# Layer 0's far entries: weighing on ScalarE, a sum over a transposed view on VectorE, and a search for the largest over four blocks at once

## The chip, the cores and the metric

The kernel runs on one core of one Trainium2 chip. The metric is device time in microseconds for one execution. The kernel before takes 1902.93 us, the median of three runs (1902.68 to 1903.74).

## The reference

Four graph layers are applied one after another to `x` (2708 nodes, 128 features), all with one adjacency `adj` (2708 x 2708). About 2.4% of the entries of `adj` are nonzero: a random symmetric pattern plus the diagonal, each entry weighted by a uniform number between 0.05 and 1. After each layer the result is added to `x` and normalized. Layer 0 is the one that is changed:

```python
s = node_feats @ msg_w[:, :D].T
d = node_feats @ msg_w[:, D:].T
messages = jax.nn.gelu(s[:, None, :] + d[None, :, :] + msg_b, approximate=False)
aggregated = jnp.einsum('ijd,ij->id', messages, adj)
combined = jnp.concatenate([node_feats, aggregated], axis=-1)
new_feats = combined @ upd_w.T + upd_b
h = jax.nn.gelu(new_feats, approximate=False) + node_feats
```

So for every pair (i, j) a vector of 128 GELUs is weighted by `adj[i, j]` and summed over j. A pair whose weight is zero adds nothing.

## The kernel before

**The two ways through layer 0.** The kernel has a sparse way, which is always run, and a dense way (`all_pairs`, from line 1082), which stands in a branch at the end of the program:

```python
    with tc.If(counts[0] > 0), ExitStack() as top:
        load_x()
        all_pairs()
        layers_1_to_3(top)
```

`counts[0]` is the number `bad_n` that the sparse way leaves behind, read by `layers_1_to_3` at its beginning. If it is above zero, then after the sparse layer 0 and layers 1 to 3 have all been run, `x` is loaded anew, layer 0 is computed over all pairs, and layers 1 to 3 are run once more on it.

**The sparse way.** The rows i are cut into `LT` = 22 tiles of `LR` = 125 rows; the columns j into `NB` = 22 blocks of `JB` = 124. For each row and block the nonzero entries are ranked by position. The first `CAP` = 5 of a block go into five slots. `slot` (L836) builds one-hot matrices `S`, `pick` (L944) uses them on TensorE to gather rows of `d` (and the weights beside them, in the last 25 columns of `dA`) into PSUM tiles `sl` (three buffers) and adds `s`; ScalarE takes the GELU (L1028); VectorE makes the weights `W` (`weigh`, L1014); TensorE sums (`add_up`, L957), two blocks at a time.

**The far entries.** What lies beyond the fifth entry of a block is "far". `past` (L864) leaves the far weights of a row in `o` (128 x 2728) and the number of far entries of each block in `count`. `largest_of` (L877) takes the 8 largest of every two blocks with VectorE's MAX8 into `cand` (11 groups of 8), `largest` (L881) takes the `OV` = 16 largest of those into `v`. `where` (L908) finds their columns, `fetch` (L912) gathers rows of `d` from HBM with 16 indirect DMAs of GpSimd, which add onto the rows of `s` that `start_far` (L903) has put into `far`. `far_gelu` (L919) takes the GELU of eight at once (128 x 1024); `far_sum` (L922) adds one weighted far entry to `extra` on VectorE; `turn` (L930) brings `extra` and the slots' sums together on TensorE, and `close` copies them to `aggT`.

**The kernel's own test for lost entries.** `check` (L889) compares, for each row, the far entries that were counted with those that came out in `v`:

```python
nc.vector.tensor_reduce(n[:, 2:3], self.count, AX.X, ALU.add)
nc.vector.tensor_tensor(n[:, 2:3], n[:, 2:3], n[:, 0:1], op=ALU.subtract)
nc.vector.tensor_tensor(bad[:, self.t:self.t + 1], n[:, 2:3], n[:, 1:2], op=ALU.add)
```

`n[:, 0]` is the number of positive values in `v`, `n[:, 1]` the number of equal neighbours among them. The sum of `bad` over all rows becomes `bad_n` (L1076).

**The order of the work.** It is written out by hand. The loop over `block` (L1021, 484 blocks) emits, for block b: `pick(b)` on TensorE, the GELU of b on ScalarE, `weigh` of block b-1 on VectorE, then the steps that are due at this block, then every second block `add_up`. Steps come from `Rows.when` (L748), sorted by their block, and within a block by tile and by place in the list. Each engine works through its instructions in this order. Counted in blocks of the tile that is being picked, the far steps of that tile fall on: `where` 1 and 3, `fetch` 2 and 11, `far_gelu` 15 for its first eight entries and 28 (that is block 6 of the next tile) for the second eight; `far_sum` two at a time on 17 to 20 and on 30 to 33 (8 to 11 of the next tile); `turn` and `close` on 36 (14 of the next). Beside them lie steps of the next tile: `rank` (a matmul by `tri`, L820, and a copy by ScalarE, L821) on 1, 3, 9, 11, 17 and 18, `part0` (L828, ScalarE) on 3, 9 and 17, `rank_row` (L861) with `past` and `largest_of` on 5, 7, 13, 15, 20 and 21. `rank`, `rank_row` and `turn` share one PSUM tile `ps` (L629, one buffer): each must wait until the one before has been read out.

**The dense way.** `all_pairs` goes through the 2708 rows one by one: a GELU of 128 x 2708 on ScalarE, then for each half of the row TensorE spreads the row of `adj` over the partitions into PSUM (`bc`, two buffers of 1354 columns), and VectorE multiplies and sums:

```python
nc.vector.scalar_tensor_tensor(
    g[:, b0:b1], g[:, b0:b1], 1.0, bc[:, :b1 - b0], op0=ALU.mult, op1=ALU.mult,
    accum_out=part[:, i, h:h + 1])
```

For every 25 rows GpSimd splits the weights into three bf16 parts (five instructions over 2708 columns).

Of the kernel before, what the change touches and what calls it, by code (L numbers as in the profile page):

```python
# [14 lines left out]
F32 = mybir.dt.float32  # L15
BF16 = mybir.dt.bfloat16
U32 = mybir.dt.uint32
AF = mybir.ActivationFunctionType
ALU = mybir.AluOpType
AX = mybir.AxisListType  # L20
PSUM = bass.MemoryType.PSUM

P = 128
# [149 lines left out]
def gnn_stack(ctx: ExitStack, tc: tile.TileContext, t, out: bass.AP):  # L173
    nc = tc.nc
    N, D = t["x"].shape
# [355 lines left out]
    NB = 22  # L531
# [12 lines left out]
    PB = BANK // P  # L544
# [7 lines left out]
    with ExitStack() as l0:  # L552
# [10 lines left out]
        with ExitStack() as msg:  # L563
# [62 lines left out]
            vp = msg.enter_context(tc.tile_pool(name="values", bufs=3))  # L626
            up = msg.enter_context(tc.tile_pool(name="sums", bufs=2))
# [110 lines left out]
            class Rows:  # L738
# [9 lines left out]
                def when(self):  # L748
                    base = (self.t - 1) * NB
                    yield base + 8, self.load_s  # L750
                    for h, (b0, b1) in enumerate(thirds):
                        b = base + b0
                        yield b - 10, lambda h=h: self.load(h)
                        yield b - 1, lambda h=h: self.find(h)
                        at = (1, 3, 5, 7) if b1 - b0 == HB else (1, 2, 4, 5)
                        for n in range(2):
                            m = 2 * h + n
                            yield b + at[n], lambda h=h, n=n: self.rank(h, n)
                            yield b - 5 + 4 * n, lambda m=m: self.load_row(m)
                            yield b + at[2 + n], lambda m=m: self.rank_row(m)  # L760
                            yield b + at[2 + n], lambda m=m: self.past(m)
                            yield b + at[2 + n], lambda m=m: self.largest_of(m)
                        yield b + 9, lambda h=h: self.part0(h)
                        yield b + 10, lambda h=h: self.part1(h)
                        for k, wait in enumerate(((12, 13, 14, 15, 16), (8, 8, 9, 11, 11), (14, 15, 16, 17, 18))[h]):
                            yield b + wait, lambda h=h, k=k: self.slot(h, k)
                    b = base + NB
                    yield b, self.largest
                    yield b + 6, self.check
                    for n in range(OV // 8):  # L770
                        yield b + 1 + n * 2, lambda n=n: self.where(n)
                    if self.t == 0:
                        b += 4
                    for n in range(OV // 8):
                        yield b - 1 + n * 9, lambda n=n: self.start_far(n)
                        yield b + 2 + n * 9, lambda n=n: self.fetch(n)
                        yield b + 15 + n * 13, lambda n=n: self.far_gelu(n)
                        for k in range(8):
                            yield b + 17 + n * 13 + k // 2, lambda n=n, k=k: self.far_sum(n * 8 + k)
                    yield b + 36, self.turn  # L780
                    yield b + 36, self.close

# [81 lines left out]
                def past(self, m):  # L864
                    if m == 0:
                        self.o = op_.tile([P, max(NB * JB, NT * D)], F32, name="o")
                        self.o = self.o[:, :NB * JB].rearrange("p (b j) -> p b j", j=JB)
                        self.cand = vp.tile([P, NB // 2, 8], F32, name="cand")
                        self.count = vp.tile([P, NB], F32, name="count")
                    b = slice(m * PB, min((m + 1) * PB, NB))  # L870
                    n = b.stop - b.start
                    nc.vector.scalar_tensor_tensor(self.o[:, b, :], self.ps[m][:, :n, :JB], EDGE + CAP,  # L872
                                                   self.ar[m][:, :n, :], op0=ALU.is_ge, op1=ALU.mult)
                    nc.vector.tensor_scalar(self.count[:, b], self.ps[m][:, :n, JB], -float(CAP), 0.0,
                                            op0=ALU.add, op1=ALU.max)

                def largest_of(self, m):  # L877
                    for b in range(m * PB, min((m + 1) * PB, NB), 2):
                        nc.vector.max(self.cand[:, b // 2, :], self.o[:, b:b + 2, :].rearrange("p b j -> p (b j)"))  # L879

                def largest(self):  # L881
                    c = self.cand.rearrange("p g e -> p (g e)")
# [36 lines left out]
                def far_gelu(self, n):  # L919
                    nc.scalar.activation(self.far[n], self.far[n], AF.Gelu)  # L920

                def far_sum(self, k):  # L922
                    w, f = self.v[:, k:k + 1], self.far[k // 8][:, k % 8, :]
                    if k == 0:
                        self.extra = up.tile([P, D], F32, name="extra")
                        nc.vector.tensor_scalar(self.extra, f, w, None, op0=ALU.mult)
                    else:
                        nc.vector.scalar_tensor_tensor(self.extra, f, w, self.extra, op0=ALU.mult, op1=ALU.add)  # L928

                def turn(self):  # L930

# [81 lines left out]
            with tc.manual_schedule():  # L1013
                def weigh(b, g, sl, W):  # L1014
                    nc.vector.tensor_tensor(  # L1015
                        W[:, :, :RG].rearrange("p (k c) i -> p k c i", k=2), columns_of(sl, D, DA),
                        own[:, None, None, :].to_broadcast([P, 2, 3, RG]), op=ALU.mult)


                late = []  # L1020
                for block in range(LT * NB):  # L1021
                    i, b = divmod(block, NB)
                    while steps and steps[0][0] < block:
                        steps.pop(0)[2]()
                    sl, W = sl_all[block % len(sl_all)], W_all[block % len(W_all)]
                    R[i].pick(b, sl)
                    g = ep.tile([P, 6, D], F32, name="g")
                    nc.scalar.activation(g.rearrange("p (k c) d -> p k c d", k=2), columns_of(sl, 0, D), AF.Gelu,  # L1028
                                         scale=1.0 / D_SCALE)
                    if late:  # L1030
                        weigh(*late[-1])
                    while steps and steps[0][0] == block:
                        steps.pop(0)[2]()
                    late.append((b, g, sl, W))
                    if len(late) == LAG + 2:
                        R[(block - LAG) // NB].add_up(late[:2])
                        late = late[2:]
                weigh(*late[-1])
                R[-1].add_up(late)


                rest = [step for _, _, step in steps]
                assert len(rest) == 11
                last_gelu, far_sums, last_turn = rest[0], rest[1:9], rest[9:]
                G = len(groups())
                ahead = LR * (LT - 1) // BANK
                U.open()
                for n in range(ahead):
                    U.sums(n)
                    if n > 0:  # L1050
                        U.rows(n - 1)
                    if n == 1:
                        last_gelu()
                    if n == 2:
                        for step in far_sums:
                            step()
                for step in last_turn:
                    step()
                U.rows(ahead - 1)

                most = vp.tile([P, 1], F32, name="most")
                ones = vp.tile([P, 1], F32, name="ones")
                fine = vp.tile([P, LT], F32, name="fine")
                nc.vector.memset(ones, 1.0)
                nc.vector.tensor_tensor(fine, tot[:, :, 0], tot[:, :, 1], op=ALU.add)
                nc.vector.tensor_tensor(fine, fine, fine, op=ALU.is_equal)
                nc.vector.tensor_tensor(bad, bad, fine, op=ALU.subtract)
                nc.vector.tensor_scalar(bad, bad, 1.0, None, op0=ALU.add)
                nc.vector.tensor_reduce(most, bad, AX.X, ALU.add)

                def between():
                    ps = p_misc.tile([P, BANK // P, P], F32, name="ps")
                    nc.tensor.matmul(ps[:1, 0, :1], ones, most, start=True, stop=True)
                    for n in range(ahead, G):
                        U.sums(n)
                    nc.vector.tensor_copy(bad_n, ps[:1, 0, :1])  # L1076
                    for n in range(ahead, G):
                        U.rows(n)

                U.norm.all(between)  # L1080
# [865 lines left out]
```

## Time and profile before

| | |
|---|---|
| median of three runs | 1902.93 us |
| profiled execution, its own time | 1905.26 us |
| its span | 1903.5 us |
| TensorE busy | 1626.2 us (85%) |
| VectorE busy | 1436.1 us (75%) |
| ScalarE busy | 1052.1 us (55%) |
| GpSimd busy | 630.8 us (33%) |
| layer 0's loop over blocks | from about 55 us to about 882 us |
| layers 1 to 3 | from about 939 us to the end |
| one tile of 22 blocks in the middle of the loop | 37.0 us |

Engines are named PE (TensorE matmul), PEld (its weight load), DVE (VectorE), ACT (ScalarE), POOL (GpSimd) and SP (SyncE). L928 is line 928 of the kernel. A group of instructions is shown as "out<-in, shape, count | busy us, mean ns of one | idle time of the engine just before them, and what ended it". Two instructions of one engine can overlap at their edges, so a group's busy time can be less than its count times the mean. No instruction of lines 1082 to 1147 is in this trace.

### The profile page before, as it was taken

What the parts mean: (1) busy time and instruction counts of PE and PEld (TensorE: products, weight loads), DVE (VectorE), ACT (ScalarE), POOL (GpSimd) and SP (SyncE); (2) the same over time, 40 slices, a digit from 0 to 9 for tenths busy, and PEclk for the clock granted to TensorE, in tenths of its full rate; (3) what the DMA queues carried; (4) which work ended last, traced back from release to release, by engine and by line L of the source; (5) the groups of instructions that cost most, each with busy time, mean ns of one, the idle gap of its engine ahead of it and who ended that gap; (6) DMA issues with size and microseconds to landing.
All of it is one profiled execution on the core that took longest, in us unless ns stands there. A gap on an engine that the chain in (4) does not pass through costs nothing.

```text
span 1903.5 us, 36624 instructions
## 1 busy us (share of the span) xinstructions
PE 1626.2 (85%) x14033; PEld 955.4 (50%) x14033; DVE 1436.1 (75%) x3607; ACT 1052.1 (55%) x1538; POOL 630.8 (33%) x426
## 2 busy tenths in 40 slices
PE   5899999999999999986599997577888897199995
PEld 5666666666666666655344443322223343044542
DVE  6899999999999999986678885838886783860104
ACT  3667667666766766654444444458886771430003
POOL 5667766776776677565100000000000000000000
PEclk8899999999999999998699998658998798599997
DMA  8666665666666576533134430032334463354431
GB/s 214 153 130 143 133 144 119 148 122 141 143 131 142 122 149 124 117 69 88 63 123 150 152 112 1 1 106 76 142 137 140 141 199 146 137 204 146 146 121 31
DMA packets 234896, 238.30 MB, mean 125 GB/s; under 512 B 28844, under 2 KB 219630, under 8 KB 228122
## 3 DMA queue, kind: packets, MB, share of 16 engines
q1 hardware_dynamic: 183670, 212.18, 36.1%
q0 software_dynamic: 51040, 23.68, 10.7%
q8 instruction: 112, 1.84, 0.4%
q14 instruction: 74, 0.61, 0.1%
HBM read 220.65 MB, written 15.15 MB: 124 GB/s over the span
## 4 chain that ended last, share of the span: by engine, by line
PE 43%; DVE 28%; POOL 8%; issue 7%; ACT 7%; DMA 5%; DVEq 0%; SPq 0%; ACTq 0%; POOLq 0%
PE acc L1843 10%; POOL far L914 8%; PE lg L1231 5%; PE acc L1238 5%; PE accV L1571 5%; DVE ix L910 5%; PE ps L1499 4%; DMA far<-d_tab,ix 3%; DVE W L1015 3%; PE sl L950 3%; DVE extra L928 2%; DVE o L872 2%; DVE S L840 2%; PE accO L1575 2%; DVE dA L833 1%
## 5 line engine op out<-in xcount | busy, mean ns | idle before, releaser
L914 POOL DMA_INDIRECT far<-d_tab,ix x352 | 563.0, 1600 | 257.5 <-DVE W L1015 110.6
L1028 ACT ACTIVATE g<-sl 128x768 f32<-128x768 f32 x484 | 393.3, 813 | 257.0 <-PE sl L955 201.0
L950 PE MATMUL sl<-dA,S 124*128 124x153 f16 x4840 | 408.2, 231 | 10.1 <-DVE W L1015 7.7
L950 PEld LDWEIGHTS <-S 124*128 124x128 f16 x4840 | 330.4, 98 | 79.7 <-issue 67.9
L966 PE MATMUL acc<-g,W 128*32 128x128 f32 x4840 | 205.5, 277 | 0.5 <-issue 0.5
L966 PEld LDWEIGHTS acc<-g,W 128*32 128x32 f32 x4840 | 140.6, 109 | 58.8 <-issue 55.5
L955 PE MATMUL sl<-s,same 50*128 50x384 f16 x968 | 161.9, 308 | 0.0
L1015 DVE TENSOR_TENSOR W<-sl,own 128x150 f32<-128x150 f32 x484 | 143.4, 300 | 14.6 <-ACT g L1028 13.4
L1232 ACT ACTIVATE w<-lg,row_L_gnn_gate_bias 128x512 f32<-128x512 f32 (+1 forms) x132 | 83.5, 636 | 108.2 <-PE lg L1231 106.9
L1486 POOL TENSOR_TENSOR arena<-arena,off 128x128 f32<-128x128 f32 (+1 forms) x22 | 21.6, 982 | 351.1 <-DMA arena<-in_adjT 321.3
L840 DVE TENSOR_SCALAR S<-rk 124x1000 f16<-124x1000 bf16 (+1 forms) x330 | 133.4, 430 | 0.0
L910 DVE FIND_INDEX8 ix<-v,o 128x8 uint32<-128x2728 f32 x44 | 131.7, 2993 | 0.0
L1571 PE MATMUL accV<-arena,X 128*128 128x512 f32 (+4 forms) x264 | 124.7, 592 | 6.5 <-DVE arena L1537 6.5
L1231 PE MATMUL lg<-qT,mT 128*128 128x512 f32 (+2 forms) x264 | 121.1, 547 | 3.6 <-ACT w L1232 3.1
L1238 PE MATMUL acc<-w,both 128*128 128x512 f32 (+2 forms) x264 | 121.2, 547 | 0.0
L928 DVE SCALAR_TENSOR_TENSOR extra<-far,v,extra 128x128 f32<-128x128 f32 x330 | 114.9, 348 | 6.3
L449 DVE TENSOR_TENSOR g<-ps,row_L_gnn_b 128x512 f32<-128x512 f32 (+2 forms) x14 | 7.9, 574 | 148.1 <-PE ps L447 148.0
L1499 PE MATMUL ps<-XT 128*128 128x512 f32 (+8 forms) x150 | 90.4, 691 | 32.2 <-ACT arena L1505 26.5
L872 DVE SCALAR_TENSOR_TENSOR o<-ps,ar 128x496 f32<-128x496 f32 x132 | 82.4, 624 | 37.0 <-issue 19.7
L1843 PE MATMUL acc<-at,x 128*128 128x512 f32 (+2 forms) x156 | 66.2, 574 | 48.4 <-ACT x L379 48.4
L1233 DVE TENSOR_TENSOR w<-w,at 128x512 f32<-128x512 f32 (+1 forms) x132 | 82.5, 625 | 27.1 <-ACT w L1232 27.1
L879 DVE MAX8 cand<-o 128x8 f32<-128x248 f32 x242 | 90.4, 411 | 0.0
(357 smaller groups left out, 2507.2 us busy)
## 6 DMA issues: line engine op xcount, KB each, us to landing
at<-in_adjT SPq DMA_DIRECT2D x42, 1354.0 KB
ar<-in_adj SPq DMA_DIRECT2D x105, 248.0 KB
far<-s_tab SPq DMA_DIRECT2D x44, 512.0 KB
at<-in_adjT SPq DMA_DIRECT2D x42, 448.0 KB
arena<-in_adjT SPq DMA_DIRECT2D x21, 704.0 KB
arena<-in_adjT SPq DMA_DIRECT2D x21, 650.0 KB
held<-in_adjT SPq DMA_DIRECT2D x7, 1354.0 KB
f_tab<-arena SPq DMA_DIRECT2D x10, 704.0 KB
```

Of the source, the lines that this page charges most:

```text
L840: nc.vector.tensor_scalar(self.S[h][:, :n, :, k * RG:(k + 1) * RG], self.rk[h][:, :n, :LR].rearrange("p b (c i) -> p b c i", c=NC), EDGE + ...
L910: nc.vector.max_index(ix, self.v[:, n * 8:n * 8 + 8], self.o.rearrange("p b j -> p (b j)"))
L914: nc.gpsimd.indirect_dma_start(out=self.far[n][:, k, :], out_offset=None, in_=d_tab[:, :], in_offset=bass.IndirectOffsetOnAxis(ap=self.ix[ ...
L950: nc.tensor.matmul(group[c], self.S[h][:, n, c, :], dA[q][:, b, c, :], start=c % 3 == 0 and q == 0, stop=False)
L966: nc.tensor.matmul(self.acc[q:q + 32, k, :], W[:, c, :], g[:, c, :], start=b == 0 and k == 0, stop=ends)
L1015: nc.vector.tensor_tensor(W[:, :, :RG].rearrange("p (k c) i -> p k c i", k=2), columns_of(sl, D, DA), own[:, None, None, :].to_broadcast([ ...
L1028: nc.scalar.activation(g.rearrange("p (k c) d -> p k c d", k=2), columns_of(sl, 0, D), AF.Gelu, scale=1.0 / D_SCALE)
L1231: nc.tensor.matmul(lg, mT[:, j * P:j * P + r], qT[:, a:b], start=True, stop=True)
L1238: nc.tensor.matmul(acc[k], mrow[:rows[j], j, :], ws[j][:rows[j], a:b], start=j == 0, stop=j == NT - 1)
L1499: nc.tensor.matmul(ps, XT[:, self.js], XT[:, c], start=True, stop=False)
L1571: nc.tensor.matmul(Pair.acc[0][:, a:b], X[:self.r, self.j, :], self.w_[:, a:b], start=first, stop=last)
L1843: nc.tensor.matmul(acc[k], src[:rows[j], j, :], at[:rows[j], a:b], start=j == order[0], stop=j == order[-1])
```

## The change

It has two parts. In the far sum, `far_weigh` multiplies one far entry in place by its weight, on ScalarE, in place of VectorE's multiply-and-add; `far_sum` then sums eight of them with one `tensor_reduce` over a view in which the entry is the innermost index, and adds the first eight's sum to the second's. `far_weigh` is due two at a time on 16 to 19 (and 29 to 32), `far_sum` on 20 (and 33). In the search, `largest_of` takes the 8 largest of four blocks (496 columns) where it took those of two, so that `cand` has 6 groups of 8 where it had 11. The tail after the loop, which names the last steps by position, is adapted.

```diff
                         yield b + 15 + n * 13, lambda n=n: self.far_gelu(n)
                         for k in range(8):
-                            yield b + 17 + n * 13 + k // 2, lambda n=n, k=k: self.far_sum(n * 8 + k)
+                            yield b + 16 + n * 13 + k // 2, lambda n=n, k=k: self.far_weigh(n * 8 + k)
+                        yield b + 20 + n * 13, lambda n=n: self.far_sum(n)
...
-                        self.cand = vp.tile([P, NB // 2, 8], F32, name="cand")
+                        self.cand = vp.tile([P, -(-NB // PB), 8], F32, name="cand")
...
                 def largest_of(self, m):
-                    for b in range(m * PB, min((m + 1) * PB, NB), 2):
-                        nc.vector.max(self.cand[:, b // 2, :], self.o[:, b:b + 2, :].rearrange("p b j -> p (b j)"))
+                    o = self.o[:, m * PB:min((m + 1) * PB, NB), :]
+                    nc.vector.max(self.cand[:, m, :], o.rearrange("p b j -> p (b j)"))
...
-                def far_sum(self, k):
-                    w, f = self.v[:, k:k + 1], self.far[k // 8][:, k % 8, :]
-                    if k == 0:
-                        self.extra = up.tile([P, D], F32, name="extra")
-                        nc.vector.tensor_scalar(self.extra, f, w, None, op0=ALU.mult)
-                    else:
-                        nc.vector.scalar_tensor_tensor(self.extra, f, w, self.extra, op0=ALU.mult, op1=ALU.add)
+                def far_weigh(self, k):
+                    f = self.far[k // 8][:, k % 8, :]
+                    nc.scalar.activation(f, f, AF.Copy, scale=self.v[:, k:k + 1])
+
+                def far_sum(self, n):
+                    part = up.tile([P, D], F32, name="extra")
+                    nc.vector.tensor_reduce(part, self.far[n].rearrange("p k d -> p d k"), AX.X, ALU.add)
+                    if n:
+                        nc.vector.tensor_tensor(part, part, self.extra, op=ALU.add)
+                    self.extra = part
...
-                assert len(rest) == 11
-                last_gelu, far_sums, last_turn = rest[0], rest[1:9], rest[9:]
+                assert len(rest) == 12
+                last_gelu, far_sums, last_turn = rest[0], rest[1:10], rest[10:]
```

## The prediction

> **What bounds the kernel now.** I read the busy shares first, then one steady tile, then its waits, then the rows that price the change. Page, part 1:
>
> ```profile
> PE 1626.2 (85%) x14033; PEld 955.4 (50%) x14033; DVE 1436.1 (75%) x3607; ACT 1052.1 (55%) x1538; POOL 630.8 (33%) x426
> ```
>
> Over the whole run VectorE is second; in layer 0's loop it stands level with TensorE. Busy time from one block 15 to the next (one tile, 22 blocks):
>
> ```profile
> core 0: us, PE busy (x) PEld busy (x) DVE busy (x) ACT busy (x) POOL busy (x), PEclk, DMA share, GB/s
> 343.20:380.20 37.00, 35.41 (x526) 25.49 (x518) 34.92 (x101) 25.40 (x38) 25.47 (x17) 1.00 0.65 135
> ```
>
> PE is free for 1.6 us of 37.0, DVE for 2.1. Both look like the bound, so the waits of that tile decide:
>
> ```profile
> DVE o L872 <- issue: 1.6, 1, 1.6
> ...
> PE ps L820 <- ACT rk L821: 1.1, 1, 1.1
> ...
> PE ps L934 <- DVE count L874: 0.3, 1, 0.3
> ...
> PEld L820 <- DVE mask L812: 0.3, 1, 0.3
> ```
>
> In the timeline PE runs from one `pick` to the next without a hole but for: 1.1 us at block 18, where the second `rank` waits until ScalarE has copied `ps` out; about 0.3 us before `pick` of block 6 (VectorE comes late from its two 3 us FIND_INDEX8); under 0.3 us at block 9 (`mask`); 0.3 to 0.4 us at `turn` (`count`). DVE in turn idles 1.6 us at block 15. So TensorE sets the pace, and VectorE costs it at most about 0.9 us per tile.
>
> The rows that price the change, by shape:
>
> ```profile
> L928 DVE SCALAR_TENSOR_TENSOR extra<-far,v,extra 128x128 f32<-128x128 f32 x330 | 114.9, 348 | 6.3
> L926 DVE TENSOR_SCALAR extra<-far,v 128x128 f32<-128x128 f32 x22 | 7.5, 339 | 0.0
> L879 DVE MAX8 cand<-o 128x8 f32<-128x248 f32 x242 | 90.4, 411 | 0.0
> L1731 DVE TENSOR_REDUCE v<-room 128x11 f32<-128x1408 f32 x3 | 4.9, 1620 | 2.4 <-ACT room L1727 2.4
> L1393 ACT ACTIVATE X<-M,w 128x128 f32<-128x128 f32 x22 | 6.8, 389 | 3.2 <-DVE w L1388 3.2
> L833 DVE SCALAR_TENSOR_TENSOR dA<-at,dA 124x1000 f16<-124x1000 f32 x44 | 52.3, 1188 | 1.1 <-ACT dA L828 1.1
> L833 DVE SCALAR_TENSOR_TENSOR dA<-at,dA 124x750 f16<-124x750 f32 x22 | 20.4, 929 | 0.0
> L920 ACT ACTIVATE far<-far 128x1024 f32<-128x1024 f32 x44 | 46.1, 1049 | 0.0
> L971 ACT ACTIVATION_READ_ACCUMULATOR agg<-acc 128x1 f32 x22 | 4.3, 194 | 0.0
> ```
>
> **What the Trainium skill says.** "ScalarE: Activation LUTs", What ACT_TABLE_LOAD costs: an ACTIVATE takes 186 ns plus 0.833 ns per column, each pointer operand adds about 93 ns, back-to-back ones overlap by about 93. For 128 columns and a pointer scale that is 386 ns; L1393, the very form of `far_weigh`, shows 389, and 6.8/22 = 0.31 us apart. "VectorE: DVE Perf Modes", The perf-mode tier table: `tensor_reduce` runs at one element a cycle only; L1731 agrees (1.62 us for 1408). "SBUF — State Buffer", Door 1, on cachelines: an access that changes its 16-byte line each time pays a penalty, size not given; no long DVE read with such a stride is in this trace. "VectorE: DVE Perf Modes", Two Vector instructions with no wait between them: an operation that writes out an accumulator is two instructions; the trace shows that on ScalarE (L971), not on VectorE.
>
> **The search first, for it can decide alone.** MAX8 gives eight values, whatever its width (128x8 from 248 columns in L879, from 88 in L885). Four blocks may hold more than eight far entries; the rest would be lost, `check` would count one more than came out, `bad_n` would be above zero, and the branch with `all_pairs` would be taken. Whether that happens is a question about the input, not about an engine. In the adjacency that the reference's setup builds I counted the far entries (nonzeros beyond the fifth of a row in a block of 124): at most 7 in any two blocks that `largest_of` takes together, at most 14 in a row, so the kernel before loses none; the trace, without an instruction of `all_pairs`, agrees. In four blocks the most is 9: row 608, blocks 16 to 19, with 0, 4, 0 and 5. One entry of that row is lost, `bad_n` is 1, and the dense way runs. One row is enough.
>
> **The change part by part, per tile.**
> - VectorE, far sum: removed (114.9 + 7.5)/22 = 5.56 us. Added two reduces of 1024: by the slope of L833, (1188 - 929)/250 = 1.036 ns per column, 1.62 - 384 x 0.001036 = 1.22 us each, and one add, 0.29 us (like L449's 282 ns for 128x128). The view's stride is the unknown: at twice the time per element a reduce would take 2.3 us, and below one element a cycle it can't go, so 1.1 (1024 x 1.036 ns) is the lower end. I take 1.22, because L833 and L1731 show that slope and no row a worse one; at 2.3 both waits below grow by 1.1 us, 2.2 per tile. Together 2.7.
> - VectorE, search: 90.4/22 = 4.11 us becomes five of 0.67 (411 + 248 x 1.036) and one of 0.41: 3.8. The second stage reads 48 columns instead of 88, three times: 0.1 less. VectorE saves 5.56 - 2.7 + 0.4 = 3.2 us of 34.9.
> - ScalarE: 16 x 0.31 = 4.9 us more, 30.3 of 37. Where: between the GELU and the later tile's `part0` and `rank` copy. On block 17 two of them (0.62) stand ahead of `part0` and of the copy that TensorE already awaits for 1.1 us: PE loses 0.6. The last pair of the first eight ends about 1.5 us after `pick(19)`; the reduce starts only then, and `past(4)`, queued behind it on VectorE, starts 2.7 us after `pick(19)` where it started 1.9: `rank_row` of block 21, which needs `ps` back, waits some 0.3, and VectorE reaches its FIND_INDEX8 and the `W` that `pick(6)` needs about 0.3 later still. The second eight: pair on block 10 ends at 375.0 by the same walk, reduce and add to 376.4, `past(2)` 0.4 later than now, `turn` with it. Sum 0.6 + 0.3 + 0.3 + 0.4, less 0.1 from the shorter search: +1.5 us per tile, some 20 tiles, +30 us. The fetch DMAs, their queue and the `far` buffers keep their blocks; `extra`'s two buffers are read before they come round. In the tail eight copies and one reduce replace eight sums (3.4 us): nothing.
> - The dense way. (a) New load of `x`, transposes and two products over all columns, with GpSimd's first split beside them: 35 us, since in the kernel's own start `x` lands at 10.5 us and its transposes and products follow at like sizes. (b) 2708 rows. VectorE, per half: 1354 columns, 1.188 + 354 x 0.001036 = 1.556 us, less 0.08 by which consecutive ones overlap in the timeline, plus the accumulator's read: bounds 0 and L971's full 194 ns; I take 0.09, what it adds on ScalarE, where the next operation starts 0.09 after the read. 1.57 a half, 3.15 a row with a little for waits. ScalarE needs about 2.5 (1.049 + 1684 x 0.00084 = 2.46, plus 0.09 for a pointer bias, less 0.09 overlap), TensorE six bf16 products (a 512-wide one takes about 0.23 in the timeline), some 1.3. GpSimd splits 25 rows in about 20 us (L1202: 6.1 us for 2816 columns, twice, and three copies at 0.9 to 1 ns a column as in L700), against 79. VectorE binds: 2708 x 3.15 = 8530 us. (c) Update and norms: in the trace 41 us from the end of the last far step to `x` complete at 939, and 6 groups of products at some 3: 60 us. (d) Layers 1 to 3 again: 1903.5 - 938.7 = 965, plus 10 for what layer 1 now does under layer 0's end: 975.
>
> Against the profiled span: 1903.5 + 30 + 35 + 8530 + 60 + 975 = 11,533 us. The profiled run's own time was 1905.26, the median 1902.93; that difference is nothing here. Forecast 11,530 us.
>
> **Rivals.**
> - No row is refused (other input than the one counted, or a test that lets it pass), and ScalarE's copies come late: +30, about 1933 us. For it: everything above on blocks 17 to 21. Against it: the count.
> - No row is refused, and the copies fit into ScalarE's 11.6 idle us per tile: then PE loses only less to VectorE, at most 0.9 x 20 = 18 us, about 1885 us. It decides if the copies of block 17 don't hold up the copy of `ps`; they stand ahead of it in the queue, so I hold it unlikely.
> - The dense way is taken, but its rows go at another pace: with 0 for the accumulator's read and full overlap 2.95 a row, 10,990 us; with 194 ns and no overlap 3.5 a row, 12,480; should the multiply with accumulation run at half rate, over 19,000.
>
> **How the numbers follow.** Dense way 0.92 (of it 0.05 outside its pace bounds), late copies 0.05, fitting copies 0.02, neither 0.01. Range 10,900 to 12,500, the two bounds with a little for (a), (c) and (d), holds 0.87 and leaves both small cases out. Faster by over 0.2% (what a measurement can tell): 0.02. Within: 0.01. Slower: 0.97.
>
> **What would show it.** The GELU and the multiply of `all_pairs`, 2708 and 5416 of them, VectorE near 100% over some 8.5 ms, and layer 1's logits twice. The first 1.93 ms keep the old form: loop tiles near 38.5 us, L820's wait on L821 about 1.7 us per tile, 352 copies of 0.39 us and 44 reduces of 1.2 us. No such lines, and a time near 1900, and the count was wrong.

## The result, and the profile after

The changed kernel takes 11,200.67 us (median of four runs, 11,197.01 to 11,213.4) against 1902.81 us: 5.888 times as long, with a 95% interval of 5.878 to 5.898. It was forecast at 11,530 us, with a range of 10,900 to 12,500. The profiled execution's span is 11,195.3 us.

In the lines of the kernel after, `far_weigh` is L925, the reduce L929, MAX8 L880, the second `rank` and its copy L821 and L822, `rank_row` L862, `past`'s `count` L875, `turn` L938, `W` L1019, and the rows of the dense way L1127 (GELU), L1131 (matmul) and L1132 (multiply and sum).

The page's busy shares first, then its groups of the dense way:

```profile
PE 9453.8 (84%) x32852; PEld 3514.6 (31%) x32852; DVE 10247.4 (92%) x15401; ACT 8539.4 (76%) x5284; POOL 2633.1 (24%) x1000
```

```profile
L1132 DVE SCALAR_TENSOR_TENSOR g<-g,bc 128x1354 f32<-128x1354 f32 x5416 | 8185.8, 1563 | 12.2 <-issue 12.2
L1131 PE MATMUL bc<-s,sel 75*128 75x512 bf16 (+1 forms) x16248 | 6976.8, 567 | 1220.3 <-DVE g L1132 1215.6
L1127 ACT ACTIVATE g<-dT,sT 128x2708 f32<-128x2708 f32 x2708 | 6911.3, 2552 | 1279.1 <-DVE g L1132 1279.1
...
L1132 DVE DVE_READ_ACCUMULATOR g<-g,bc 128x1 f32 x5416 | 448.8, 83 | 0.0
```

The lines of `all_pairs`, absent before, are there with 2708 and 5416 instructions. VectorE idles for 12.2 us in all of them, while TensorE and ScalarE each wait some 1,200 us for VectorE: VectorE sets the pace of the dense way. One row and a half of it in the timeline (start, duration, then the instruction):

```profile
4998.69 1.57 DVE L1132 SCALAR_TENSOR_TENSOR g<-g,bc 128x1354 f32<-128x1354 f32 x1
4998.82 2.55 ACT L1127 ACTIVATE g<-dT,sT 128x2708 f32<-128x2708 f32 x1 [0.47 <-DVE g L1132]
...
5000.19 0.08 DVE L1132 DVE_READ_ACCUMULATOR g<-g,bc 128x1 f32 x1
5000.19 1.56 DVE L1132 SCALAR_TENSOR_TENSOR g<-g,bc 128x1354 f32<-128x1354 f32 x1
...
5001.67 0.08 DVE L1132 DVE_READ_ACCUMULATOR g<-g,bc 128x1 f32 x1
5001.72 1.57 DVE L1132 SCALAR_TENSOR_TENSOR g<-g,bc 128x1354 f32<-128x1354 f32 x1
```

The next multiply starts with the accumulator's read, or 0.05 us after it, and the read itself begins before the multiply ends: 1.50 and 1.53 us from start to start.

The whole span adds up from the trace's time marks (the last part of `x` by its start, as for the 938.7 us of the kernel before):

| stretch | measured, us | forecast, us |
|---|---|---|
| first pass, to its first output DMA | 1961.4 | 1933.5 (to the end of its span) |
| `x` again, transposes, two products, to the first L1132 (1997.5) | 36.1 | 35 |
| 2708 rows, to about 10,190 | 8192.6 | 8530 |
| update and norms, to the last part of `x` (10,233.4) | 43.3 | 60 |
| layers 1 to 3 again, to the end | 961.9 | 975 |

The changed code of layer 0 itself, in the first pass (groups of the first 1960 us, shapes kept apart):

```profile
L925 ACT ACTIVATE far<-far,v 128x128 f32<-128x128 f32 x352 | 120.6, 396 | 0.0
L929 DVE TENSOR_REDUCE extra<-far 128x128 f32<-128x1024 f32 x44 | 85.8, 1950 | 12.3 <-ACT far L925 10.2 <-issue 2.1
L880 DVE MAX8 cand<-o 128x8 f32<-128x496 f32 x110 | 74.6, 678 | 0.0
```

The weighing (0.396 us) and the search (0.678 us) cost what was forecast; the reduce takes 1.95 us, not 1.22. TensorE's waits in one steady tile (from 405.5 to 445.4; line waited at, released by, us in total, times, longest):

```profile
PE ps L821 <- ACT rk L822: 1.7, 1, 1.7
PE ps L862 <- DVE count L875: 0.9, 1, 0.9
PE ps L938 <- DVE count L875: 0.8, 1, 0.8
PE sl L954 <- DVE W L1019: 0.6, 2, 0.4
```

These are the four places that the forecast named, 4.0 us in place of the 1.6 us before. But tiles of the changed kernel aren't alike. From one `turn` to the next, in three tiles (duration, busy time of PE, PEld, DVE, ACT and POOL with counts, TensorE's granted clock, DMA share, GB/s):

```profile
402.40:442.39 39.99, 35.87 (x519) 25.56 (x519) 34.57 (x83) 29.66 (x55) 26.17 (x17) 1.00 0.62 125
442.39:482.40 40.01, 35.79 (x519) 25.54 (x519) 34.44 (x83) 29.64 (x55) 25.82 (x16) 1.00 0.60 125
482.40:523.50 41.10, 37.24 (x518) 26.32 (x518) 33.91 (x82) 29.30 (x54) 26.15 (x17) 0.96 0.62 122
```

The third one is 1.1 us longer, at a mean clock of 0.96. In half microseconds (same columns), the clock falls 0.1 us after TensorE has resumed from the wait for `rank`'s copy:

```profile
490.50:491.00 0.50, 0.00 (x0) 0.00 (x0) 0.28 (x1) 0.50 (x2) 0.50 (x1) 1.00 0.16 19
491.00:491.50 0.50, 0.29 (x5) 0.05 (x7) 0.50 (x1) 0.50 (x2) 0.50 (x1) 0.80 0.37 46
491.50:492.00 0.50, 0.50 (x13) 0.47 (x16) 0.50 (x2) 0.50 (x2) 0.45 (x1) 0.50 0.32 39
...
494.50:495.00 0.50, 0.50 (x7) 0.29 (x6) 0.00 (x0) 0.17 (x1) 0.50 (x1) 0.79 0.86 134
495.00:495.50 0.50, 0.50 (x11) 0.37 (x8) 0.00 (x0) 0.50 (x1) 0.50 (x1) 1.00 0.94 212
```

A clock of 0.80 in a half microsecond means that its last 0.2 us ran at half speed; so the half clock lasts from about 491.3 to 494.7 us, 3.4 us. The kernel before has about 37.04 us in each of its steady tiles, at 1.00.

### The profile page after: what moved, and what is told of

The parts are those of the page before. It is cut to its first block, busy times and chain, and to the rows that moved or that the text cites. A ratio compares the mean times of both kernels' runs of the same rounds, so it can differ in the third digit from the quotient of the medians.

```text
span 11195.3 us, 96724 instructions
## 1 busy us (share of the span) xinstructions
PE 9453.8 (84%) x32852; PEld 3514.6 (31%) x32852; DVE 10247.4 (92%) x15401; ACT 8539.4 (76%) x5284; POOL 2633.1 (24%) x1000
## 5 line engine op out<-in xcount | busy, mean ns | idle before, releaser
L1132 DVE SCALAR_TENSOR_TENSOR g<-g,bc 128x1354 f32<-128x1354 f32 x5416 | 8185.8, 1563 | 12.2 <-issue 12.2
L1131 PE MATMUL bc<-s,sel 75*128 75x512 bf16 (+1 forms) x16248 | 6976.8, 567 | 1220.3 <-DVE g L1132 1215.6
L1127 ACT ACTIVATE g<-dT,sT 128x2708 f32<-128x2708 f32 x2708 | 6911.3, 2552 | 1279.1 <-DVE g L1132 1279.1
L1131 PEld LDWEIGHTS <-sel 75*128 75x128 bf16 x16248 | 2168.9, 134 | 6027.8 <-issue 5918.5
L1120 POOL CAST s<-a 75x2708 bf16<-75x2708 f32 x109 | 265.7, 2437 | 6450.0 <-PE bc L1131 6139.0
L1122 POOL TENSOR_TENSOR a<-a,s 50x2708 f32<-50x2708 f32 x218 | 1163.0, 5335 | 17.6
L1123 POOL CAST s<-a 50x2708 bf16<-50x2708 f32 x218 | 529.9, 2431 | 14.0
L1132 DVE DVE_READ_ACCUMULATOR g<-g,bc 128x1 f32 x5416 | 448.8, 83 | 0.0
L1575 PE MATMUL accV<-arena,X 128*128 128x512 f32 (+1 forms) x528 | 246.7, 587 | 13.0 <-DVE arena L1541 13.0
L1235 PE MATMUL lg<-qT,mT 128*128 128x512 f32 (+1 forms) x528 | 242.3, 547 | 7.3 <-ACT w L1236 6.3
```

The costliest lines, as they stand in the source:

```text
L1122: nc.gpsimd.tensor_tensor(a[:n, :], a[:n, :], s[:n, :], op=ALU.subtract)
L1123: nc.gpsimd.tensor_copy(s[:n, :], a[:n, :])
L1127: nc.scalar.activation(g, dT, AF.Gelu, bias=sT[:, i:i + 1])
L1131: nc.tensor.matmul(bc[:, c0 - b0:c1 - b0], one, s[:, c0:c1], start=True, stop=True)
L1132: nc.vector.scalar_tensor_tensor(g[:, b0:b1], g[:, b0:b1], 1.0, bc[:, :b1 - b0], op0=ALU.mult, op1=ALU.mult, accum_out=part[:, i, h:h + 1])
L1235: nc.tensor.matmul(lg, mT[:, j * P:j * P + r], qT[:, a:b], start=True, stop=True)
```

## The experiments

What was to be settled: is it the search over four blocks that brings the dense way, and through which rows; and, with the dense way out of the picture, what the other edits cost in layer 0, where the first pass came out at +66 us and not at +30.

**The search in pairs, the other edits kept** (`far_pairs`).

```diff
-                    o = self.o[:, m * PB:min((m + 1) * PB, NB), :]
-                    nc.vector.max(self.cand[:, m, :], o.rearrange("p b j -> p (b j)"))
+                    for b in range(m * PB, min((m + 1) * PB, NB), 2):
+                        nc.vector.max(self.cand[:, b // 2, :], self.o[:, b:b + 2, :].rearrange("p b j -> p (b j)"))
...
```

> The changed kernel with the search put back to two blocks at once; the far weighing on ScalarE and the transposed sum stay. Theory (one entry lost in the four-block search sends the kernel through the dense way): no instruction of all_pairs, 1962 us, which is where the first pass ends in the changed kernel's trace, give or take 3. Rival (something in the new far sum makes bad_n positive): the dense way again, 11,200 us.

Measured: 1975.65 us, ratio 1.0373 [1.0356, 1.0391], and no instruction of `all_pairs`. So without the four-block search the dense way isn't taken, and the change is still slower by 3.7%. The time is some 14 us above what was expected: the expectation took the first pass of the changed kernel to end at its last `x`, without the output's way out, and counted that kernel's shorter search too.

**The search over four blocks alone, in the kernel before** (`search4`): the reverse edit.

> The kernel before with the search over four blocks alone. Theory (the lost entry): the dense way, with a first pass like the kernel before's, 11,200 - 60 = 11,140 us. Rival (the far sum is the cause): no dense way, 1895 to 1903 us.

Measured: 11,133.87 us in a single execution, dense way taken; 67 us below the changed kernel. The search alone makes the factor of 5.9, and the rest of the change the other 67 us.

**Only blocks 16 to 19 as two pairs** (`split16`), the other four-block groups as in the change.

```diff
...
+                    parts = [(m * PB, min((m + 1) * PB, NB), m)]
+                    if m == 4:
+                        parts = [(m * PB, m * PB + 2, m), (m * PB + 2, (m + 1) * PB, -(-NB // PB))]
...
```

> The changed kernel in full, except that the group of blocks 16 to 19 is searched as two pairs; the other five groups stay at four blocks (the last at two). Theory (row 608, blocks 16 to 19, is the only place with more than eight far entries): no dense way, 1962 us, within 3 of far_pairs. Rival (other rows or groups lose entries as well): the dense way, 11,200 us.

Measured: 1973.77 us, ratio 1.0367 [1.0350, 1.0384], no dense way. One group of blocks is responsible. The count of the input in the forecast had named it: row 608 with 0, 4, 0 and 5 far entries in blocks 16 to 19. The runs show the group of blocks; that it is one row and one entry stands on the count alone.

**The reduce over eight elements side by side** (`far_flat`; as `far_pairs`, but what is added up isn't the eight entries of one feature).

```diff
-self.far[n].rearrange("p k d -> p d k")
+self.far[n].rearrange("p k d -> p (k d)").rearrange("p (d k) -> p d k", k=8)
```

> far_pairs with the sum over eight neighbouring elements in place of the transposed view: as many elements, no stride; it sums the wrong elements, so layer 0's far part is not computed. Theory (the stride makes the reduce 1.95 us instead of 1.22, and both reduces hold up TensorE by what they are late): reduce 1.22 us, tile 1.46 us shorter, 1962 - 29 = 1933 us. Rival (only ScalarE's place in the queue holds things up, the reduce is covered): within 5 us of far_pairs. Rival (the reduce takes 1.95 us whatever its view): no change either, with the reduce at 1.95.

Measured: 1936.98 us, ratio 1.0178 [1.0161, 1.0195]. Its group of the reduce, against 1980 ns in `far_pairs`:

```profile
L929 DVE TENSOR_REDUCE extra<-far 128x128 f32<-128x1024 f32 x44 | 53.7, 1220 | 12.2 <-ACT far L925 8.8 <-issue 3.4
```

Same operation, same shape, same count: the stride of 512 bytes alone costs 0.73 to 0.76 us per reduce, and 38.7 us of the time. Of the 1.85 us per steady tile (41.0 to 39.15 in the mean), 1.5 are there at whole clock too (40.15 to 38.63); the rest is the clock, which falls in fewer tiles. Both figures of the forecast's bracket are now placed: 1.22 us is the price side by side, and 1.95 lies near the end at twice the time per element (2.3).

**Weighings behind the other steps of their block** (`far_behind`; as `far_pairs`, but ScalarE copies `ps` for `rank` before it weighs).

```diff
-yield b + 16 + n * 13 + k // 2, lambda n=n, k=k: self.far_weigh(n * 8 + k)
+yield b + 16.5 + n * 13 + k // 2, lambda n=n, k=k: self.far_weigh(n * 8 + k)
```

> far_pairs with the 16 weighings of a tile moved to the end of their block's steps, so that on block 17 the two stand behind part0 and the copy of ps, not ahead of them. Theory (the copies ahead of the copy of ps cost TensorE 0.6 us per tile): the wait of L821 on L822 falls from 1.7 to 1.1 us per tile, 1975 - 21 x 0.6 = 1963 us. Rival (what is late is only the reduce, so TensorE loses the same a little further on): 1975 us.

Measured: 1955.26 us, ratio 1.0276 [1.0259, 1.0293]: 20.4 us less than `far_pairs`, and some 8 us below what was expected. The wait for `rank`'s copy is back at 1.1 us. The trace shows what the rest is. In `far_pairs` the steady tiles take 40.15 to 40.2 us where the clock stays whole and about 41.6 where it falls, 41.0 in the mean of 16; in `far_behind` 14 of 16 take 39.75, and two 41.25. So the waits gave back about 0.4 us per tile, and the clock about 0.6.

**Three contiguous adds in place of the reduce** (`far_tree`; as `far_pairs`).

```diff
-nc.vector.tensor_reduce(part, self.far[n].rearrange("p k d -> p d k"), AX.X, ALU.add)
+f = self.far[n]
+nc.vector.tensor_tensor(f[:, 0:4, :], f[:, 0:4, :], f[:, 4:8, :], op=ALU.add)
+nc.vector.tensor_tensor(f[:, 0:2, :], f[:, 0:2, :], f[:, 2:4, :], op=ALU.add)
+nc.vector.tensor_tensor(part, f[:, 0, :], f[:, 1, :], op=ALU.add)
```

> far_pairs with the transposed reduce replaced by three adds over contiguous halves (4, 2 and 1 entries of 128, in place). Theory (it is the reduce's length that stands in TensorE's way): three adds take 0.69 + 0.42 + 0.29 less overlaps, 1.24 us in place of 1.98, so about as far_flat, 1937 to 1945 us. Rival (length doesn't matter, only the wait for ScalarE): 1975 us.

Measured: 1955.11 us, ratio 1.0273 [1.0256, 1.0290], 10 us above the upper end. The adds take 0.69, 0.43 and 0.29 us, 1.41 in all, 0.2 above the contiguous reduce's 1.22, and its tiles at whole clock take 39.15 to 39.5 us. But 11 of 16 steady tiles have the half clock, and the mean is 40.07.

**Both** (`tree_behind`).

> Search in pairs, the reduce replaced by three contiguous adds, and the weighings put behind the other steps of their blocks. If ScalarE's lateness at block 17 (worth 20 us alone) and VectorE's longer chain (worth 20 us alone with the adds) are two separate terms, they add: 1975.7 - 20.4 - 20.5 = 1935 us (1931 to 1940). Rival: both were the same slack, released once: 1950 to 1956 us.

Measured: 1937.06 us, ratio 1.0174 [1.0157, 1.0191]. The sum is the expected one, but not for the expected reason. All 16 steady tiles are at 1.00, and they take about 39.05 us: 0.1 less than the undisturbed ones of `far_tree`. TensorE's waits from 200 to 800 us:

```profile
PE ps L821 <- ACT rk L822: 17.2, 16, 1.1
PE ps L941 <- DVE count L875: 16.0, 15, 1.1
PE ps L862 <- DVE count L875: 9.8, 15, 0.8
PE sl L957 <- DVE W L1022: 6.8, 30, 0.6
```

Putting the weighings behind hence gained almost nothing in waits here (what `rank` no longer waits, `rank_row` and `turn` wait): nine tenths of the gain is the clock. That the two figures added is luck: what was expected to add were two waits.

**The half clock over all runs.** Where the wait for `rank`'s copy is about 1.65 us, the half clock follows it 13 times of 18 in the changed kernel, 10 of 18 in `far_pairs`, 8 of 18 in `far_flat`, 13 of 18 in `far_tree`. Where the wait is about 1.1 us, in the kernel before, `far_behind` and `tree_behind`, it follows it never (17, 18 and 18 waits).

The traces show what picks the 44 of these 72 waits, each a hole in TensorE's work. In each trace, all changes of the clock lie on one grid of 3.413 us, to within 0.02 us. A hole that lies within one interval of the grid was followed by the half clock 43 times of 48; one that lies across a grid point, 1 time of 24. The five exceptions of the 48 began within 0.25 us after a grid point, and the one of the 24 ended on one. Two tiles of the changed kernel, in intervals of its grid (columns as above):

```profile
446.93:450.34 3.41, 2.64 (x37) 1.75 (x28) 2.74 (x10) 3.36 (x8) 3.06 (x2) 1.00 0.62 113
450.34:453.75 3.41, 2.53 (x41) 1.84 (x41) 2.35 (x4) 2.78 (x7) 2.80 (x3) 1.00 0.44 55
...
487.89:491.30 3.41, 1.76 (x19) 1.03 (x16) 2.19 (x7) 3.36 (x8) 2.80 (x3) 1.00 0.51 105
491.30:494.71 3.41, 3.41 (x33) 2.23 (x32) 1.59 (x4) 1.41 (x4) 2.80 (x3) 0.50 0.41 53
```

In the first tile the hole (449.6 to 451.2) is shared by two intervals, which keep 2.64 and 2.53 us of TensorE; in the second it lies whole in one, which keeps 1.76, and the next interval runs at half clock. The Trainium skill, "TensorE: Matmul & The Clock Gate", Part 1 on the HAM clock gate, says that the clock knows two states, half and full, that it falls after an idle window of 3413 ns, and that this window runs freely. The 0.50, the 3.4 us and the free run agree. That a whole idle window is needed doesn't: windows in which TensorE was busy for half of the time were enough. The share isn't a sharp bound: in `far_behind`, the half clock at 438.5 us came after three microseconds in each of which TensorE was busy for some 0.6, and other windows like it brought none.

**The kernel before, with `part0` elsewhere.** Three runs asked what the 1.1 us wait of the kernel before is worth, for the forecast had read from it that TensorE sets the pace. `part0_late` puts the second `part0` two blocks later and its `part1` with it:

```diff
-yield b + 9, lambda h=h: self.part0(h)
+yield b + (9, 11, 9)[h], lambda h=h: self.part0(h)
-yield b + 10, lambda h=h: self.part1(h)
+yield b + (10, 12, 10)[h], lambda h=h: self.part1(h)
```

> The kernel before with part0 and part1 of the second third two blocks later (19 and 20 in place of 17 and 18), so that the copy of ps on block 17 follows ScalarE's GELU at once. Theory (TensorE sets the pace and stands 1.1 us per tile for that copy): 1903 - 21 x 1.0 = 1882 us. Rival (VectorE sets the pace, it was busy 34.9 of 37.0 us): 1898 to 1903 us.

Measured: 1911.99 us, ratio 1.0048 [1.0031, 1.0064]. Slower: both the theory and the rival (1898 to 1903) failed. TensorE's waits of 200 to 800 us, where the kernel before has 18.5 at `rank`, 6.0 at `turn` and 0.2 at `sl`:

```profile
PE sl L950 <- DVE W L1015: 9.6, 32, 0.6
PE ps L861 <- DVE count L874: 9.2, 16, 0.6
PE ps L934 <- DVE count L874: 6.1, 16, 1.4
```

The wait for `rank` is gone, and the waits for `count` and `W` have come in its place: VectorE's 1.2 us of `part1` now stand ahead of them. `part0_early` moves only the second `part0`, one block ahead (`(9, 8, 9)[h]`):

> The kernel before with one edit: the second part0 (ScalarE's copy and weighing of the middle third of a tile's adjacency) a block earlier, so that it no longer stands ahead of ScalarE's copy that the second rank waits for. Theory 'both engines bind in turn': the rank wait of 1.1 us per tile goes or halves, but VectorE's own chain from past(3) to the W that pick(6) needs stays whole and keeps most of the tile, so 1895 to 1903 us. Rival 'TensorE alone sets the pace': the whole wait comes off, 20 x 1.0, 1880 to 1885 us.

Measured: 1901.20 us, ratio 0.9985 [0.9979, 0.9992], the only version below the kernel before, and by less than the 0.2% that count here. The wait for `rank` falls from 18.5 us to 5.5, `W` and `count` bring 9 us of new ones, and a tile takes 36.95 us. `balanced` goes on from there, and moves VectorE's far sums of four entries out of blocks 17 to 20:

```diff
-yield b + 17 + n * 13 + k // 2, lambda n=n, k=k: self.far_sum(n * 8 + k)
-                    yield b + 36, self.turn
...
+at = (17 + k // 2 if k < 4 else 26 if self.t == 0 else 30) if n == 0 else 33 + k // 2
+yield b + at, lambda n=n, k=k: self.far_sum(n * 8 + k)
+                    yield b + 38, self.turn
...
```

> The kernel before with the second part0 a block earlier and four of VectorE's eight far sums of the first eight moved out of the blocks 15 to 20 into the later half of the tile (with the second eight and the turn shifted behind them). Theory 'both engines bind in turn': VectorE's chain between blocks 15 and 5 is 4 x 0.35 = 1.4 us shorter and the rank wait is smaller, so some 1.0 us per tile comes off: 1883 us (1875 to 1890). Rival: the later half of the tile has no room on VectorE either and the turn moves by what was put before it, 1900 us or more.

Measured: 1905.38 us, ratio 1.0012 [1.0001, 1.0022]. Also a miss, and the rival (1900 us or more) holds: TensorE now waits hardly anywhere but at `turn` (18.7 us in 16 waits for `count`), and the tile takes 37.1 us. A wait of about 1.1 us per tile has come back at the next place where TensorE needs something of VectorE. In these 600 us VectorE is busy for 574.4 us, TensorE for 574.7, 96% each: both are nearly full.

**The change made to fit.** `best` joins `far_tree`, `far_behind`, `part0_late` and later sums (blocks 26 and 37) with `turn` on 38; it was meant to beat both kernels.

> far_tree with part0 of the second third late as in part0_late, the weighings behind their block's other steps, the first eight's sum moved from block 20 to 26, the second eight's sum from 33 to 37 and turn and close from 36 to 38. Theory (TensorE's own work is 35.0 us per tile, the rest is waits on ps and W that ScalarE and VectorE can be kept out of): 35.3 us per tile, 1903 - 21 x 1.7 = 1867 us. Rival (ScalarE's 4.9 us more per tile always comes in TensorE's way somewhere): 1885 us or more, not better than part0_late.

Measured: 1942.15 us, ratio 1.0200 [1.0182, 1.0217], 75 us off; what its rival said (1885 us or more) holds. It had `part0_late` in it, which costs by itself; its steady tiles take 39.3 us, and TensorE waits 17.9 us for `count` at `turn`, 9.1 at `rank_row` and 15.6 for `W` in 200 to 800 us. `far_balanced` takes `part0` early instead, the weighings 1.5 blocks later than the change has them, and sums on blocks 8 and 14 of the next tile:

```diff
-yield b + 16 + n * 13 + k // 2, lambda n=n, k=k: self.far_weigh(n * 8 + k)
-yield b + 20 + n * 13, lambda n=n: self.far_sum(n)
-                    yield b + 36, self.turn
...
+yield b + 17.5 + n * 13 + k // 2, lambda n=n, k=k: self.far_weigh(n * 8 + k)
+yield b + ((26 if self.t == 0 else 30) if n == 0 else 36), lambda n=n: self.far_sum(n)
+                    yield b + 38, self.turn
...
```

> Search in pairs, three contiguous adds in place of the reduce, second part0 a block earlier, weighings behind the other steps of their blocks, the first eight's sum moved from block 20 to block 8 of the next tile, the second's sum and the turn two or three blocks later. If VectorE's relief in the far sum (5.56 us per tile removed, about 3 added) is real time once neither engine waits on ScalarE at block 17 and the sum is off the chain between blocks 15 and 5: 1870 to 1885 us. Rival: ScalarE's sixteen weighings still make the W of the blocks wait for their GELU, and the time stays near tree_behind's 1935 us or above.

Measured: 1911.04 us, ratio 1.0044 [1.0027, 1.0061]. That is 26 us below `tree_behind`, but neither the 1870 to 1885 us of the theory nor the rival's 1935. Its tiles take 37.5 us at whole clock. TensorE waits at one place, and VectorE waits for ScalarE (200 to 800 us):

```profile
PE ps L941 <- DVE count L875: 27.3, 16, 2.0
```

```profile
DVE W L1022 <- ACT g L1035: 35.8, 59, 1.0
```

VectorE's far sums take 3.1 us per tile in place of 5.6, but its instructions overlap at their edges, and its busy time per tile falls only from 35.0 to 33.7 us; it is busy for 540 us of the 600, no longer full. But `W` of a block waits for that block's GELU, ScalarE's sixteen weighings make the GELUs later, and `count`, which stands behind those `W` in VectorE's queue, comes to `turn` 1.7 us late. So the load taken off VectorE came back as ScalarE's lateness. Whether a later `turn` still would take the rest off wasn't tried. The 18 holes of 1.6 to 2.0 us at `turn` bring no half clock in this run, and the grid says why: each of them lies across a grid point. This tile of 37.5 us is 11 intervals of 3.413 (37.55) long, so the next hole meets the grid at nearly the same place. One of them, from 381.2 to 382.7 us:

```profile
378.67:382.08 3.41, 2.50 (x32) 1.71 (x28) 3.31 (x11) 2.37 (x4) 2.94 (x2) 1.00 0.66 110
382.08:385.50 3.42, 2.76 (x38) 2.19 (x38) 3.42 (x12) 1.73 (x3) 2.81 (x3) 1.00 0.57 114
```

## Why the prediction was right, and where its steps were off

- **The count decides.** Right, and shown from both sides: `search4` takes the dense way with nothing but the search changed, `split16` avoids it by splitting the one group that holds row 608's nine.
- **The rows, 3.15 us each.** 8192.6 us over 2708 rows are 3.025. The term that was off is the accumulator's read, 0.09 us in the sum: the record takes 83 ns, but half a row takes 1.512 us from start to start, so with the multiply's 1.563 and the forecast's overlap of 0.08 it adds 0.03. 337 us of the total came from there. ScalarE's 2.5 us per row was right (2.552). TensorE's 1.3 wasn't: 6976.8 / 2708 = 2.58, at a granted clock of 0.50 through the whole stretch; it stayed hidden under VectorE's 3.02, by 0.4 us. GpSimd's 20 us for 25 rows are 18.0 (2.44 + 2 x (5.34 + 2.43)), hidden too.
- **Update and norms, 60 us.** 43.3: the 41 us from the last far step to `x` in the kernel before were a good measure alone; what the forecast put on top for the products wasn't there. The start was right (36.1 for 35). Layers 1 to 3 took 961.9 for 975: the 965 of the kernel before held, and the 10 us on top for work under layer 0's end didn't show.
- **The first pass, +30 us.** +66 at layer 0's end (938.7 to 1004.5 us). The step that failed is the price of the reduce, "I take 1.22": it was the contiguous price, and the view has a stride. The forecast had written down what a dearer one does (both waits grow by the difference): 2 x (1.95 - 1.22) = 1.46 us per tile on top of 1.5, together 2.96; measured at whole clock 39.98 - 37.04 = 2.94. With the contiguous reduce of `far_flat` it is 38.63 - 37.04 = 1.59 against the 1.5, and its waits in one such tile grow by 0.6 us at `rank`, 0.2 at `rank_row`, 0.4 at `W` and 0.3 at `turn`, where the forecast had 0.6, 0.3, 0.3 and 0.4. So the walk through blocks 17 to 21, the copy of `rank` at 1.7 us included, was right. That both waits grow by the whole difference is only half shown: from that tile to the one of the changed kernel, `rank_row` grows by 0.7, `W` and `turn` by 0.2 each. What the forecast had no term for is the clock: 11 of 16 steady tiles lose 1.1 us to it, 0.76 in the mean. The 16 steady tiles so make (2.94 + 0.76) x 16 = 59 of the 66 us, and the tiles at the loop's ends the rest.
- **"TensorE sets the pace, and VectorE costs it at most about 0.9 us per tile."** Too simple. `part0_late`, `part0_early` and `balanced` show that behind the wait at `rank` stands one for VectorE of about the same size. This didn't touch the forecast, since the change made the waits longer, but it made the rival of 1885 us look nearer than it was.
- **The rivals.** "Late copies without the dense way", 1933: had no row lost an entry, it would have been 1974 to 1976 (`split16`, `far_pairs`), the size off by the reduce and the clock. "Fitting copies", 1885: no run came near; the best made of the change is 1911.
- **What the skill said of the reduce.** "VectorE: DVE Perf Modes", The perf-mode tier table, gave one element a cycle, and the 1.22 us of `far_flat` agree. "SBUF — State Buffer", Door 1, gave a penalty for each new 16-byte line without its size; here the stride costs 0.73 us for 1024 elements, 60% on top; whether new lines are the reason, or another cost of the stride, no run separates. The forecast named it and then priced it at zero; the middle of its bracket would have been nearer.

## What to carry to other kernels

Before a cheaper search or a wider tile is priced in time, count in the input what it must hold: one row with nine entries where eight fit costs here 9.2 ms, nearly five times the whole kernel. Price a strided read by the time of a strided read, and an operation moved to a less busy engine by what its queue lets through behind it. Where two engines are both full, a wait that is taken away comes back at the next meeting point; look at the tile's period, not at the wait.

## What the runs showed of the hardware

- TensorE's clock can halve for 3.4 us after a hole of only 1.65 us, and that costs mostly 0.7 to 1.5 us of a 40 us tile; where the same hole is 1.1 us long, it didn't. In the loop it halved where a hole of 1.65 us fell whole into one interval of a grid of 3.413 us (43 of 48), and hardly ever where the hole lay across a grid point (1 of 24, and 0 of 18 with holes of 1.6 to 2.0 us). This is read from the traces; no run moved a hole on purpose.
- Through 8 ms of the dense way the clock was granted at 0.50 although TensorE's records cover 85% of it (6812.7 of 8000 us); why it wasn't released isn't settled.
- A reduce of 128 x 1024 f32 takes 1.22 us contiguous and 1.95 to 1.98 us with 512 bytes from element to element; three contiguous adds of halves do the same sum in 1.41 us.
